# A lightning-attention and router kernel: token normalisation moved to VectorE and one step sooner, decay masks, one tile's router logits and the first head weights moved to other places in the order

## The chip, the cores and the metric

The kernel runs on one core of a Trainium2 chip. A core has a matrix engine (TensorE, "PE" in the profile, its weight loads "PEld"), VectorE ("DVE"), ScalarE ("ACT"), GpSimd ("POOL") and SyncE ("SP"), whose queue issues nearly all DMAs here. The engines run at the same time; each takes its own instructions strictly in the order of the program and waits by semaphores for the others. The metric is the device time of one execution in microseconds (us), as the median of three runs; lower is better.

## The reference, cut to what matters

Tokens are x (4 batches of 512, 512 features each), 16 heads of width 128.

```python
xn = layernorm(x)                                  # per token, no weights
q, k, v = split(silu(xn @ w_qkv.T))                # per head
for block in blocks_of_64:                         # causal, with a decay s per head
    o  = (q * exp(-s*(i+1))) @ kv + ((q @ k.T) * exp(-s*(i-j)) [i>=j]) @ v
    kv = exp(-s*64) * kv + (k * exp(-s*(63-i))).T @ v
o = norm_w * o / rms(o)
s_out = (sigmoid(xn @ w_gate.T) * o) @ w_out.T
p = softmax(xn @ router_w.T + router_b); w8, i8 = top_k(p, 8)
g = silu(xn * sum(w8) + w8 @ expert_bias[i8])
out = x + s_out * g
```

## The kernel before, in words

The program's order is written out by hand: no scheduler moves anything, so an engine's queue is exactly the order in which the functions below are called.

**Tiles and units.** The four batches form two pairs p (batches 2p and 2p+1), and 512 tokens are four tiles t of 128. So there are eight tile pairs (p, t), in the order (0,0) ... (0,3), (1,0) ... (1,3); the text numbers them 0 to 7 and writes x_n, xf_n, pt_n, lg_n for what belongs to tile pair n. The first stage computes v = silu(xn @ w_v) in 16 units k = 0 to 15: units 0 to 7 take the tile pairs with the weights of the first eight heads, units 8 to 15 take them again with those of the last eight heads, the second pair of batches first. After that come 48 head units (gate, then query and key, for each pair of batches), in which the attention of the head before is interleaved, and then the output projection.

**A unit** is a product of 2x2 blocks. `plain_unit` (units 0 and 1) does it with eight block products in four steps of two; `unit` (L480 to L517) does it with seven products (`PRODUCTS`) on sums and differences of blocks: A11·B11, S2·T2, S1·T1, A12·B21, S3·T3, S4·B22, A22·T4. A is the weight side and B the token side. These products share three accumulators in PSUM (a fourth buffer lets the next unit start). VectorE has to read an accumulator before TensorE adds to it again:

```python
            elif i == 1:
                add(temp("a"), ps, s["s1"])
            elif i == 2:
                add(temp("e"), ps, s["a"])
```

So S3·T3, which goes into the accumulator of S2·T2, waits for the addition a; S4·B22, which goes into that of S1·T1, waits for the addition e; and A22·T4 waits for the addition that follows S3·T3.

**Precision.** Each 32-bit operand is split into a high half (a rounding copy on ScalarE, `split_hi`, L100) and a low half (source minus high half, `split_lo`, L103, on VectorE or GpSimd). Each block product is then six matmuls of 128x512: two chunks of the contraction, each high·high, high·low, low·high.

**What is prepared beside the units.** `after[i]` is a list of functions that are called behind product i of the running unit, so their instructions stand there in every queue. For the tile pair of the next unit and the one after it these are: `stats` (mean and variance on VectorE, 1/std by a power on GpSimd, L234 or L238), `norms` (`normalise_x`: in place in the x tile), `turn` (eight TensorE transposes into PSUM, L262, and the copies to xf on ScalarE, L263), `sums` (four subtractions on GpSimd, L277), `plain` and `more` (the splits of the token blocks B and T, high on ScalarE, low on GpSimd), and `logits` (16 small router matmuls, L323, and an addition on VectorE, L326). In unit k they are placed as follows: `turn`, `sums`, `plain`, `more`, `logits` of tile pair k+1, `stats` and `norms` of tile pair k+2. The transposes of the next unit's tile pair thus stand right behind the first product of a unit.

`normalise_x` has two forms. Tile pairs 0 and 1 are normalised on VectorE by one instruction per batch (`normalise`, L204). The other six take a small VectorE instruction for -mean/std (`shift`, L246) and then the scaling on ScalarE (L249).

**The weights of the v stage.** `sum_of` (L441) forms S1 to S4 on VectorE from the raw weights, `split_one` splits them (in `w_A_v` and `w_S_v`). The first set is made during units 0 and 1, the second during units 3 to 8. The tiles of the sums first hold the decay tables `mkdecay` of the heads: ScalarE makes them (`make_decays`, L168), GpSimd masks them (`mask_decays`, L172), and SyncE's queue stores them to DRAM (L177); four heads share one sum's tile, and a sum can be written only when the stores of its four tables have landed.

**The weights of the heads.** The last lines of the loop open the buffers of the head stage in the space of the v stage's buffers (`vs_stack.close()`), load the raw weights of the first two head units (L421), and place the first head unit's sums and splits behind the products of unit 15 (`weight_steps`).

Of the kernel before, what the change touches and what calls it, by code (L numbers as in the profile page):

```python
# [8 lines left out]
F32 = mybir.dt.float32  # L9
F32R = mybir.dt.float32r  # L10
AF = mybir.ActivationFunctionType
ALU = mybir.AluOpType
AX = mybir.AxisListType

P = 128
# [35 lines left out]
def kernel(  # L51
# [13 lines left out]
    nc = tc.nc  # L65
# [12 lines left out]
    def pool(stack, name, bufs=1, **kw):  # L78
        return stack.enter_context(tc.tile_pool(name=name, bufs=bufs, **kw))
# [10 lines left out]
    small = pool(ctx, "small", 4)  # L90
# [75 lines left out]
    def make_decays(d, hs):  # L166
        for h in hs:
            nc.scalar.activation(d[h // 4][:, h % 4], dist, AF.Exp, scale=slopes[:, h : h + 1])  # L168

    def mask_decays(d, hs):  # L170
        for h in hs:
            nc.gpsimd.affine_select(  # L172
                d[h // 4][:, h % 4, 0], d[h // 4][:, h % 4, 0], pattern=[[1, P]],
                compare_op=ALU.is_ge, fill=0.0, base=0, channel_multiplier=-1,
            )
        for h in hs:
            nc.sync.dma_start(out=decay_d[h], in_=d[h // 4][:, h % 4])  # L177


    stats = [const.tile([P, NT, 2], F32, tag=f"stats{b}", name=f"stats{b}") for b in range(B)]  # L180
    rstd_of = [const.tile([P, NT, PB], F32, tag=f"rstd{p}", name=f"rstd{p}") for p in range(B // PB)]
    rstd = [rstd_of[b // PB][:, :, b % PB] for b in range(B)]
# [20 lines left out]
    def normalise(dst, src, b, t):  # L203
        nc.vector.tensor_scalar(  # L204
            dst, src, stats[b][:, t, 0:1], rstd[b][:, t : t + 1], ALU.subtract, ALU.mult
        )
# [8 lines left out]
    xts = {}  # L215
# [7 lines left out]
    def layer_norms(p, t, apart=False):  # L223
        var = small.tile([P, PB], F32, tag="lnvar", name=f"lnv_{p}_{t}")
        for j in range(PB):
            b = p * PB + j
            st = small.tile([P, nc.vector.BN_STATS_DIM], F32, tag="bn", name=f"bn_{b}_{t}")
            nc.vector.bn_stats(st, xts[b, t])
            nc.vector.bn_aggr(stats[b][:, t, :], st)
            nc.vector.tensor_scalar(  # L230
                var[:, j : j + 1], stats[b][:, t, 1:2], 1.0, LN_EPS, ALU.mult, ALU.add
            )
            if apart:
                nc.gpsimd.tensor_tensor(  # L234
                    rstd_of[p][:, t, j : j + 1], var[:, j : j + 1], mhalf[:, 0:1], ALU.pow
                )
        if not apart:
            nc.gpsimd.tensor_tensor(rstd_of[p][:, t], var, mhalf[:, 0:PB], ALU.pow)  # L238

    def normalise_x(p, t, vector=False):  # L240
        for b in range(p * PB, p * PB + PB):
            if vector:
                normalise(xts[b, t], xts[b, t], b, t)
                continue
            shift = small.tile([P, 1], F32, tag="shift", name=f"shift_{b}_{t}")
            nc.vector.scalar_tensor_tensor(  # L246
                shift, stats[b][:, t, 0:1], -1.0, rstd[b][:, t : t + 1], ALU.mult, ALU.mult
            )
            nc.scalar.activation(  # L249
                xts[b, t], xts[b, t], AF.Identity, bias=shift, scale=rstd[b][:, t : t + 1]  # L250
            )

    xfs = {}

# [295 lines left out]
    def nothing():  # L550
        return [[] for _ in PRODUCTS]
# [262 lines left out]
    NP_FIRST = 2  # L814

    def prepare(stage, p, t):
        first = (p, t) == (0, 0)
        early = p == 0 and t < NP_FIRST

        def turn():  # L820
            for j in range(PB):
                transpose(stage, p, j, t)
            if p == 0:
                nc.sync.dma_start(out=xf_d[t], in_=xfs[p, t])

        if p == 0 and t < NP_FIRST:
            sums = (lambda: plain(p, t, nc.vector if t == 0 else nc.gpsimd)), lambda: None, lambda: None
        else:
            sums = combine(stage, p, t, nc.gpsimd)

        def route_logits():
            logits(stage, p, t)
        return {
            "stats": lambda: layer_norms(p, t, first), "norms": lambda: normalise_x(p, t, early),
            "turn": turn, "sums": sums[0], "plain": sums[1], "more": sums[2], "logits": route_logits,
        }

# [14 lines left out]
    def weight_steps(w, after):  # L852
        for i in range(4):
            after[i // 2].append(lambda i=i: w.sum_of(i, nc.gpsimd))

        def split(i):
            if i == 0:
                w.parts = w.splits((nc.gpsimd,) * 4)
            w.parts[i]()
        for i in range(4):  # L860
            after[2 + i].append(lambda i=i: split(i))

    def load_pair(stage, p, t):
        for j in range(PB):
            load_x(stage, p * PB + j, t)
# [5 lines left out]
    stage = right(vs_stack, "stage", 4)  # L871
# [3 lines left out]
    tiles = [(p, t) for p in range(NP) for t in range(NT)]  # L875
    again = [(p, t) for p in reversed(range(NP)) for t in range(NT)]
    n1 = len(tiles)
    prep = [prepare(stage, p, t) for p, t in tiles]
# [18 lines left out]
    for n in ["A21"] + [n for n, _, _, _ in PRODUCTS]:  # L897
# [3 lines left out]
    ds = [  # L901
        sump.tile([P, KC * VW], F32, tag=f"sum{i}", name=f"mkdecay_{i}").rearrange(
            "p (h a m) -> p h a m", a=2, m=P
        ) for i in range(4)
    ]
    hs = range(0, 7), range(7, 12), range(12, NH)
# [13 lines left out]
    ws[0].split_one("A21", nc.vector)  # L920
    make_decays(ds, hs[1])
    prep[1]["norms"]()
    ws[0].split_one("A22", nc.gpsimd)
    make_decays(ds, hs[2])

    for k, (p, t) in enumerate(tiles + again):
        g, after = k // n1, nothing()
        for unit_of, what in ((n1 - 3, (0, "top")), (n1 - 2, (0, "less")), (n1 + 2, (1, "top")), (n1 + 3, (1, "less"))):
            if k == unit_of:
                after[2].append(lambda what=what: scores_less(*what))  # L930
        if n1 - NT <= k < n1:
            after[6].append(lambda p=p, t=t: keep_blocks(p, t))
        if k + 1 < n1:
            after[0 if k else 1].append(prep[k + 1]["turn"])
            if k + 3 < n1:
                after[0].append(lambda k=k: load_pair(stage, *tiles[k + 3]))
            after[1].append(prep[k + 1]["sums"])
            if k + 2 < n1:
                after[1].append(prep[k + 2]["stats"])
                after[5].append(prep[k + 2]["norms"])  # L940
            after[1].append(prep[k + 1]["plain"])
            after[4].append(prep[k + 1]["more"])
            after[4].append(prep[k + 1]["logits"])
        if k == 0:
            after[1].append(lambda: mask_decays(ds, [*hs[1], *hs[2]]))
        if k < NP_FIRST:
            for i in range(2 * k, 2 * k + 2):
                after[2 + 2 * (i % 2)].append(lambda i=i: ws[0].sum_of(i, nc.vector))
            for i, n in enumerate((("S1", "S2"), ("S3", "S4"))[k]):
                eng = nc.gpsimd if i else nc.vector  # L950
                after[2 * i + 3].append(lambda n=n, eng=eng: ws[0].split_one(n, eng))
        if k == NP_FIRST:
            after[0].append(ws[1].load())
        if n1 - 5 <= k < n1 - 1:
            after[3].append(lambda n=k - n1 + 5: ws[1].sum_of(n, nc.vector))
        for n, unit_of, step, eng, piece in (
            ("A11", n1 - 2, 6, nc.gpsimd, None), ("S2", n1 - 1, 0, nc.gpsimd, None),
            ("S1", n1 - 1, 1, nc.gpsimd, None), ("A12", n1 - 1, 2, nc.vector, 0),
            ("S3", n1 - 1, 3, nc.gpsimd, None), ("A12", n1 - 1, 4, nc.vector, 1),
            ("S4", n1, 2, nc.vector, 0), ("S4", n1, 3, nc.vector, 1), ("A22", n1, 0, nc.gpsimd, None),  # L960
        ):
            if k == unit_of:
                after[step].append(lambda n=n, eng=eng, piece=piece: ws[1].split_one(n, eng, piece))
        if n1 <= k < n1 + NT:
            after[0].append(lambda t=t: load_xf(stage, t))
        if n1 < k <= n1 + NT:
            sums, split_plain, split_sums = combine(stage, 0, k - n1 - 1, nc.gpsimd, "r")
            after[1] += [sums, split_plain]
            after[4].append(split_sums)
        if k == n1 + NT + 1:  # L970
            after[1].append(scores_exp)
        if k == 2 * n1 - 1:
            vs_stack.close()
            todo = [(p, *u) for p in range(NP) for u in h_units(p, hw_stack)]
            todo[0][3].load()()
            todo[1][3].load()()
            weight_steps(todo[0][3], after)
        v_unit(p, g, t, ws[g], vout, after, k < NP_FIRST)
    do_deferred()
# [33 lines left out]
    for i, (p, kind, n, w) in enumerate(todo):  # L1013
        after = nothing()
# [148 lines left out]
```

## Time and profile before

| what | value |
|---|---|
| median of three runs | 1091.9 us (1091.29 to 1092.09) |
| the profiled execution: its time | 1092.31 us |
| its span, first to last instruction | 1090.4 us |
| TensorE busy | 1069.5 us, 98% of the span, 5762 instructions |
| VectorE, ScalarE, GpSimd busy | 678.5, 488.7 and 720.1 us |
| mean granted TensorE clock | 0.996 of full speed |

The span and the time outside it (1.9 us) come from one execution. Busy shares are averages over stages, and an engine that is busy 98% of the time has little to lose in waits; the places where TensorE stands still can be counted one by one in the timeline. Units 0 to 15 take the first 201 us of the span.

### The profile page before, as it was taken

To read this page: it belongs to the slowest core of one execution; us is meant where nothing else is said; L and a number is where in the kernel's file an instruction comes from. 1 tells how busy PE (TensorE), PEld (TensorE's weight loads), DVE (VectorE), ACT (ScalarE), POOL (GpSimd) and SP (SyncE) were. 2 spreads that over 40 slices of the span, in tenths; PEclk is the share of its full clock that TensorE was granted. 3 is DMA by queue.
4 is the path that set the end of the run, shared out by engine and by line. 5 is a ranking of instruction groups with operands and counts; after the bars stand their busy time and mean duration, and the time that the engine had idled before them with its cause. 6 is when DMAs were issued, how large, how long until landed. Compare 5 with 4: busy or idle time off the path is not lost.

```text
span 1090.4 us, 16500 instructions
## 1 busy us (share of the span) xinstructions
PE 1069.5 (98%) x5762; PEld 912.5 (84%) x5762; DVE 678.5 (62%) x1059; ACT 488.7 (45%) x950; POOL 720.1 (66%) x725
## 2 busy tenths in 40 slices
PE   8899999999999999999999999999999999999998
PEld 7677788788888888888888888888888888788886
DVE  5677876567776655655646556556566575854554
ACT  7555555444444444444444444444444444321311
POOL 5777794777677786787777767867777756722130
PEclk9999999999999999999999999999999999999999
DMA  7465743532224223324732232223222428354351
GB/s 243 170 213 198 259 170 127 187 113 97 69 87 136 92 83 109 100 89 145 277 113 82 83 120 89 82 84 97 91 82 83 131 81 266 110 176 164 116 175 57
DMA packets 105058, 143.08 MB, mean 131 GB/s; under 512 B 9104, under 2 KB 53264, under 8 KB 104080
## 3 DMA queue, kind: packets, MB, share of 16 engines
q1 hardware_dynamic: 104112, 141.33, 39.2%
q8 instruction: 45, 0.74, 0.3%
q10 hardware_dynamic: 864, 0.70, 0.2%
q14 instruction: 37, 0.30, 0.1%
HBM read 91.14 MB, written 50.86 MB: 130 GB/s over the span
## 4 chain that ended last, share of the span: by engine, by line
PE 87%; DVE 3%; issue 1%; ACT 1%; POOL 0%; DVEq 0%; ACTq 0%; POOLq 0%
PE u_qk L505 27%; PE po L806 16%; PE u_g L505 14%; PE u_v L505 8%; PE sa L674 5%; PE o L711 5%; PE ss L697 4%; PE o L713 4%; PE kt L677 2%; PE pu L766 1%; DVE q L561 0%; PE ssq L738 0%; DVE k L561 0%; DVE w_S_v L103 0%; POOL sqs L723 0%
## 5 line engine op out<-in xcount | busy, mean ns | idle before, releaser
L806 PE MATMUL po<-wr,yr 128*128 128x512 f32 x768 | 181.1, 394 | 1.5 <-DVE u L800 1.5
L806 PEld LDWEIGHTS po<-wr,yr 128*128 128x128 f32 x768 | 144.8, 189 | 33.2 <-ACT yr L100 1.9
L505 PE MATMUL u_qk<-blk_T,ws_qk 128*128 128x512 f32 x576 | 150.2, 400 | 0.0
L723 POOL TENSOR_TENSOR sqs<-sqs,sq 128x512 f32<-128x512 f32 x60 | 77.3, 1288 | 91.4 <-ACT sq L722 89.8
L505 PEld LDWEIGHTS u_qk<-blk_T,ws_qk 128*128 128x128 f32 x576 | 104.8, 189 | 20.8
L701 DVE SCALAR_TENSOR_TENSOR st<-st,bdecay,ss 128x128 f32<-128x128 f32 x128 | 44.4, 348 | 106.2 <-ACT st L699 104.0
L505 PE MATMUL u_qk<-blk_B,wa_qk 128*128 128x512 f32 x384 | 100.7, 397 | 0.0
L103 DVE TENSOR_TENSOR yr<-yin,yr 128x512 fp32r<-128x512 f32 x64 | 69.2, 1116 | 46.5 <-ACT yr L100 44.6
L103 POOL TENSOR_TENSOR ws_qk<-sum_qk,ws_qk 128x512 fp32r<-128x512 f32 x64 | 87.9, 1384 | 14.6 <-ACT ws_qk L100 14.5
L711 PE MATMUL o<-at,vin 128*128 128x128 f32 x512 | 88.3, 274 | 0.0
L505 PEld LDWEIGHTS u_qk<-blk_B,wa_qk 128*128 128x128 f32 x384 | 71.0, 188 | 15.3
L711 PEld LDWEIGHTS o<-at,vin 128*128 128x128 f32 x512 | 77.3, 191 | 5.5
L505 PE MATMUL u_g<-blk_T,ws_g 128*128 128x512 f32 x288 | 78.4, 407 | 0.0
L683 ACT ACTIVATE kd<-kt,kdecay 128x384 f32<-128x384 f32 x64 | 37.2, 582 | 90.3 <-PE kt L677 90.3
L713 PE MATMUL o<-qd,st 128*128 128x128 f32 x384 | 74.2, 275 | 0.0
L715 DVE SCALAR_TENSOR_TENSOR y<-o,nw,gt 128x512 f32<-128x512 f32 x64 | 47.9, 749 | 40.8 <-PE o L713 39.6
L674 PEld LDWEIGHTS sa<-q,k 128*128 128x128 f32 x512 | 66.8, 191 | 7.6 <-DVE q L561 2.0
L558 ACT ACTIVATE sg_k<-k 128x512 f32<-128x512 f32 x64 | 40.5, 633 | 65.3 <-DVE k L496 65.3
L770 POOL TENSOR_TENSOR u<-u,sgu 128x512 f32<-128x512 f32 x16 | 20.7, 1292 | 73.5 <-ACT sgu L769 60.2
L674 PE MATMUL sa<-q,k 128*128 128x128 f32 x512 | 67.7, 275 | 1.2 <-DVE q L561 1.1
L685 POOL TENSOR_TENSOR qd<-q,dec 128x384 f32<-128x384 f32 x64 | 65.5, 1025 | 0.0
L722 ACT ACTIVATE sq<-o 128x512 f32<-128x512 f32 x60 | 35.9, 598 | 62.7 <-DVE y L715 58.1
(184 smaller groups left out, 2455.2 us busy)
## 6 DMA issues: line engine op xcount, KB each, us to landing
v<-vo_v SPq DMA_DIRECT2D x64, 256.0 KB, 2.1
raw_qk<-in_w_head_dram SPq DMA_DIRECT2D x64, 256.0 KB, 3.7
vin<-v SPq DMA_DIRECT2D x64, 256.0 KB, 3.3
y<-y SPq DMA_DIRECT2D x64, 256.0 KB, 2.1
yin<-y SPq DMA_DIRECT2D x64, 256.0 KB, 3.5
x<-in_x_dram SPq DMA_DIRECT2D x32, 256.0 KB, 4.9
raw_g<-in_w_head_dram SPq DMA_DIRECT2D x32, 256.0 KB, 3.2
raw_v<-in_w_v_dram SPq DMA_DIRECT2D x16, 256.0 KB, 5.7
```

The costliest lines, as they stand in the source:

```text
L103: eng.tensor_tensor(lo, src, hi.bitcast(F32), ALU.subtract)
L505: nc.tensor.matmul(ps, lhsT, rhs, start=(first and c == 0 and n == 0), stop=(c == KC - 1 and n == len(PASSES) - 1), skip_group_check=not f ...
L558: nc.scalar.activation(sg, src, AF.Sigmoid)
L674: nc.tensor.matmul(pa[:, c], k[:, c], q[:, c], start=True, stop=True)
L685: nc.gpsimd.tensor_tensor(qd[s], q[:, 1:], d[:, 1, None, :].to_broadcast([P, NT - 1, P]), ALU.mult)
L697: nc.tensor.matmul(ps[:, c], kd[s][:, c], v_of(b, h, c), start=True, stop=True)
L701: nc.vector.scalar_tensor_tensor(r[:, c], r[:, c - 1], bdecay[:, h : h + 1], ps[:, c], ALU.mult, ALU.add)
L711: nc.tensor.matmul(o, v_of(b, h, c), at[s][:, c], start=True, stop=(c == 0))
L713: nc.tensor.matmul(o, st[s][:, c - 1], qd[s][:, c - 1], start=False, stop=True)
L715: nc.vector.scalar_tensor_tensor(y, po, nw[:, h : h + 1], gts[s], ALU.mult, ALU.mult)
L723: nc.gpsimd.tensor_tensor(sq[b], sq[b], s1, ALU.add)
L806: nc.tensor.matmul(pos[t], yr[:, yi, bass.ts(t, P)], wos[h][:, wi], start=(h == 0 and n == 0), stop=(h == NH - 1 and n == len(PASSES) - 1),)
```

## The change

1. `normalise_x` always uses VectorE (`normalise`); the form with `shift` and ScalarE goes. For tile pairs 2 to 7, `norms` moves from `after[5]` to `after[4]` of unit k, ahead of `more` and `logits`.
2. The masks and the stores of the decay tables of heads 7 to 15 move from unit 0 (behind its step of two products) to before the units: those of heads 7 to 11 ahead of the low half of A22, those of heads 12 to 15 behind it. The loads of x_3 are called ahead of them (in SyncE's queue these loads stay where they were), and nine stores now stand ahead of the first two stores of unit 0.
3. The router logits of tile pair 1 move in unit 0 from `after[4]` to `after[6]`, behind the unit's last two products.
4. The low half of S4 of the second weight set moves in unit 8 from behind products 2 and 3 to behind products 0 and 1.
5. The head stage's buffers are opened, and the first two head units' raw weights loaded, in unit 14; the first head unit's sums and splits stay in unit 15.

```diff
-    def normalise_x(p, t, vector=False):
+    def normalise_x(p, t):
         for b in range(p * PB, p * PB + PB):
-            if vector:
-                normalise(xts[b, t], xts[b, t], b, t)
-                continue
-            shift = small.tile([P, 1], F32, tag="shift", name=f"shift_{b}_{t}")
-            nc.vector.scalar_tensor_tensor(
-                shift, stats[b][:, t, 0:1], -1.0, rstd[b][:, t : t + 1], ALU.mult, ALU.mult
-            )
-            nc.scalar.activation(
-                xts[b, t], xts[b, t], AF.Identity, bias=shift, scale=rstd[b][:, t : t + 1]
-            )
+            normalise(xts[b, t], xts[b, t], b, t)
...
     prep[1]["norms"]()
+    load_pair(stage, *tiles[3])
+    mask_decays(ds, hs[1])
     ws[0].split_one("A22", nc.gpsimd)
     make_decays(ds, hs[2])
+    mask_decays(ds, hs[2])
...
-            if k + 3 < n1:
+            if 0 < k < n1 - 3:
                 after[0].append(lambda k=k: load_pair(stage, *tiles[k + 3]))
             after[1].append(prep[k + 1]["sums"])
             if k + 2 < n1:
                 after[1].append(prep[k + 2]["stats"])
-                after[5].append(prep[k + 2]["norms"])
+                after[4].append(prep[k + 2]["norms"])
             after[1].append(prep[k + 1]["plain"])
             after[4].append(prep[k + 1]["more"])
-            after[4].append(prep[k + 1]["logits"])
-        if k == 0:
-            after[1].append(lambda: mask_decays(ds, [*hs[1], *hs[2]]))
+            after[4 if k else 6].append(prep[k + 1]["logits"])
...
-            ("S4", n1, 2, nc.vector, 0), ("S4", n1, 3, nc.vector, 1), ("A22", n1, 0, nc.gpsimd, None),
+            ("S4", n1, 0, nc.vector, 0), ("S4", n1, 1, nc.vector, 1), ("A22", n1, 0, nc.gpsimd, None),
...
-        if k == 2 * n1 - 1:
+        if k == 2 * n1 - 2:
             vs_stack.close()
             todo = [(p, *u) for p in range(NP) for u in h_units(p, hw_stack)]
             todo[0][3].load()()
             todo[1][3].load()()
+        if k == 2 * n1 - 1:
             weight_steps(todo[0][3], after)
```

More of the change, by code (lines that the diff above doesn't have):

```diff
@@ L817, in prepare @@
         first = (p, t) == (0, 0)
-        early = p == 0 and t < NP_FIRST
         def turn():
@@ L833, in prepare @@
         return {
-            "stats": lambda: layer_norms(p, t, first), "norms": lambda: normalise_x(p, t, early),
+            "stats": lambda: layer_norms(p, t, first), "norms": lambda: normalise_x(p, t),
             "turn": turn, "sums": sums[0], "plain": sums[1], "more": sums[2], "logits": route_logits,
```

## The prediction

> **What bounds the kernel now.** I read the page's busy line first, then TensorE's waits, then its timeline, then those of the engines that it waits for. Lines of the page and of TensorE's waits (sum, times, longest, in us):
>
> ```profile
> PE 1069.5 (98%) x5762; PEld 912.5 (84%) x5762; DVE 678.5 (62%) x1059; ACT 488.7 (45%) x950; POOL 720.1 (66%) x725
> ...
> PE pt L262 <- ACT x L249: 7.2, 6, 3.2
> PE lg L323 <- ACT xf L263: 1.9, 2, 1.5
> ...
> PE u_v L505 <- DVE w_S_v L103: 0.9, 2, 0.7
> PE u_g L505 <- POOL wa_g L103: 0.7, 1, 0.7
> ```
>
> TensorE sets the end; whatever it does not wait for is worth nothing. Nearly all its waits are in the v stage, and the largest name the normalised x. The timeline of TensorE (start, length; the end of the one before can overlap) prices them:
>
> ```profile
> 20.04 1.53 PE L537 MATMUL d_v<-w_A_v,blk_T 128*128 128x512 f32 x6
> 23.04 2.00 PE L323 MATMUL lg<-rw,xf 128*128 128x64 f32 x16 [1.47 <-ACT xf L263]
> ...
> 29.04 1.52 PE L537 MATMUL d_v<-w_A_v,blk_T 128*128 128x512 f32 x6
> 33.81 1.97 PE L262 MATMUL pt<-ident,x 128*128 128x128 f32 x8 [3.25 <-ACT x L249]
> ...
> 46.15 1.52 PE L505 MATMUL u_v<-w_A_v,blk_B 128*128 128x512 f32 x6
> 49.06 1.36 PE L262 MATMUL pt<-ident,x 128*128 128x128 f32 x8 [1.39 <-ACT x L249]
> ...
> 128.72 1.57 PE L505 MATMUL u_v<-w_S_v,blk_T 128*128 128x512 f32 x6
> ```
>
> Six 128x512 matmuls take 1.36 us start to start, so each stall is the distance between two starts less 1.36: lg_1 23.04-20.04 gives 1.64; pt_2 33.81-29.04 gives 3.41; pt_3 1.55; pt_4 to pt_7, read in the same way (62.38-60.27, 75.82-73.59, 89.25-87.03, 102.52-100.46), 0.75+0.87+0.86+0.70 = 3.18. Unit 8: from S3's start at 128.72 to the next unit's at 134.76 is 6.04 where three products take 4.08: 1.96. First gate unit: 2.34 for a first product of 1.40 and 3.10 for the next two, of 2.80: 1.24. One more cost has no wait beside it: by windows (PE, PEld, DVE, ACT, POOL busy, then clock, DMA)
>
> ```profile
> 29.97:33.39 3.42, 0.59 (x3) 0.17 (x1) 2.42 (x5) 0.45 (x1) 1.00 (x5) 1.00 0.81 265
> 33.39:36.80 3.41, 2.99 (x11) 2.76 (x12) 0.14 (x1) 3.01 (x5) 1.32 (x2) 0.50 0.83 303
> ```
>
> the granted clock falls to 0.50 right behind pt_2's stall. From 33.81 to 41.62 lie the transposes (1.12 elsewhere) and 24 matmuls (5.44): 7.81 instead of 6.56, so 1.25.
>
> All that the change can reach is 1.64+3.41+1.25+1.55+3.18+1.96+1.24 = 14.2 us.
>
> **The change part by part.**
>
> *lg_1 behind the unit's last products.* It goes to a place where xf_1 (ready 23.47) has long been copied: TensorE reaches it at 21.41+2.72 = 24.1. A22 now follows at 21.41; its low half on GpSimd ended at 21.12. Gain 1.64.
>
> *Masks.* Five masks at 0.245 us (nine took 2.25) come in front of that low half. GpSimd was idle from 16.99 to 18.58, until A22's high half was cast, and ScalarE has made these five tables by 17.57; they end at 18.2, hidden. Without that gap A22 would wait up to 1.2. The other four (1.0 us) fall into 21.12 to 23.85, also idle. The nine stores take 0.40 to 0.49 each of SyncE's queue, at about 19.4 to 23.7 instead of 29.04 to 33.29; behind them the store of the first v tile leaves a microsecond late (23.8 for 22.77), and its buffer is not written again before 33. What goes is VectorE's wait of 1.97 for its second weight sum (`mkdecay`, until 30.97).
>
> *x_2.* VectorE's order is now: S1's low half (ends 28.80), normalise twice, the second sum. 1/std is there at 28.76. One normalisation took 0.54, so the two batches are ready at 29.4 and 29.85 instead of 34.47. TensorE, 1.64 earlier, would be free at 30.40-1.64 = 28.76: 0.65 of 3.41 stays, gain 2.76. With no stretch of TensorE nearly idle for 3.4 us the slow clock goes too. The Trainium skill ("TensorE: Matmul & The Clock Gate", Part 1) says that an idle window of about 3.4 us puts TensorE at half rate for the next, on windows that run freely: by that rule 1.7 lost and gained, by the rows 1.25. I take 1.25. A later half-clock window (910.6) depends on where windows fall; I count nothing for it.
>
> *x_3 to x_7.* Each pair of `shift` (0.38 on average) and of scalings (0.80 on ScalarE) becomes a pair of normalisations on VectorE one product earlier. In units 3 to 6 VectorE was idle for 1.14 just there (before the addition behind S4·B22), x is ready some 3 us before its transposes, and the accumulators that the delayed additions free are not wanted for 3 more. So 3.18, and up to 1.55 in unit 2.
>
> *What comes next there* is GpSimd and VectorE in units 1 to 3. GpSimd worked from S2's low half (35.48) to T2's of tile pair 3 (59.6) with 1.66 idle: 22.5 us. S2's low half now starts at 29.8+1.22 (sum)+1.05 (cast) = 32.1, so T2 is ready at 54.6. Unit 3 starts, with all gains, at 60.27-7.20 = 53.07 and wants T2's low half 1.36+1.12+0.23 later, at 55.8. Here a rule speaks against the change: the Trainium skill ("SBUF — State Buffer", "SBUF: two separate sides") says that VectorE, when it reads through two ports, and GpSimd hold one port pair exclusively, for a whole instruction. The row of the only normalisations that ran beside GpSimd:
>
> ```profile
> L204 DVE TENSOR_SCALAR u<-x,stats,rstd x16: 533/538/1510, 922.4 to 1067.5; 128x512 f32<-128x512 f32 x16
> ```
>
> The median 0.54 is a free one, the 1.51 one that waited. By the median alone GpSimd loses nothing and T2 is in time; by the rule each of four normalisations takes some 0.4 from GpSimd, T2 comes at 56.2. And it waits for GpSimd in turn: x_3 stands behind the sum (1.23), the cast (1.05) and S3's two low halves (1.9) from 36.3 on, is ready between 41.5 (free) and 43.2 (each waits once), and is wanted at 41.8 and 42.4. Loss 0 to 3 in all. VectorE's 42 products of two SBUF tiles in this stage took 0.68 to 1.78, 0.91 on average, those with one tile in PSUM never over 0.70; that is nearer to the rule than to no lock, so I take 1.5. By the median alone the sum below would be 11.6.
>
> *S4 in unit 8.* VectorE, its row and the two beside it:
>
> ```profile
> 127.90 0.68 DVE L496 TENSOR_TENSOR a_v<-u_v,s_v 128x512 f32<-128x512 f32 x1
> 128.68 0.69 DVE L496 TENSOR_TENSOR e_v<-u_v,a_v 128x512 f32<-128x512 f32 x1
> 129.29 3.33 DVE L103 TENSOR_TENSOR w_S_v<-sum_v,w_S_v 128x512 fp32r<-128x512 f32 x2
> ```
>
> The two pieces, 1.65 each beside a busy GpSimd, now stand ahead of a and ahead of e. VectorE comes to them at 127.98, GpSimd is in S3's low half until 129.13, so the first ends at about 129.7, a at 130.3, the second at 131.5, e at 132.1. S3·T3 waits for a: 130.3 instead of 128.72. S4·B22 waits for e: 132.2. A22 ends at 134.9, where the unit ended at 134.76. The stall is not removed but moves from S4 to S3, because a is late next. Bounds: 0.9 lost (both pieces at 1.76 and no overlap) to 1.96 gained; I take 0.
>
> *Head weights.* Four loads (0.42 each) leave at 184.3 instead of 193.79, ahead of one store of v, which comes 1.5 later and whose buffer is free until 194. They land near 188; GpSimd, idle until 198.00, makes the sums; ScalarE casts wa_g behind its copy that ends at 194.05, and the low half is ready near 196, wanted at 201.9. Gain 1.24.
>
> **Sum**, against the profiled execution's 1092.31: 1.64+2.76+1.25+1.55+3.18+0+1.24-1.5 = 10.1, so 1082.2. It lies 0.4 above the runs' median, which gives 1091.9-10.1 = **1081.8 us**, 0.9% faster.
>
> **The rivals.**
>
> *Everything goes.* No lock, and S4's pieces are early enough: 14.2 at most, 12.6 without the 0.65 and half of the S4 term: 1079.3. For it: most rows at free durations. Against: a cannot be earlier than the piece ahead of it. Chance 0.15.
>
> *Waits that take the place of the ones removed.* In units 1 to 6 the low halves on GpSimd, held up by VectorE's new reads, become the bound, and transposes or products wait for them: pt_3's 1.55 and half of the 3.18 stay under other names, and 1.5 more is lost than I take. Left 10.1-1.55-1.6-1.5 = 5.45: 1086.4. For it: GpSimd was busy 18.34 of 20 us between 40 and 60. Against: idle stretches of 3 to 3.7 us per unit from unit 3 on. This is also the case in which the change does not do what it says. Chance 0.2.
>
> *Slower.* A normalisation stands in VectorE's queue ahead of additions that free accumulators, and waits for 1/std from GpSimd. In units 3 to 6 1/std was ready 2.1 us ahead of that place (68.73 for 70.9), and the additions have 3.1 more. If GpSimd's chain came 7 us later each time, each of six units would lose 1.8, 10.8 in all, and cancel the 10.1; at 8 us it is 6x2.8 = 16.8 and the time 1098.6. The deciding point is a 1/std that lands 7 us later against VectorE; the profile shows locks of 0.5 to 1.2. Chance 0.05.
>
> **How the numbers follow.** Forecast as summed (8 to 12 us): 0.58; everything goes 0.15; other waits 0.2; slower 0.05; no difference 0.02. What a measurement here can tell from no change is about 0.2%, 2.2 us. Faster: 0.58+0.15+0.2 = 0.93; same 0.02; slower 0.05. The range: down to 14.2 less the fixed 0.65, 1078.3, and up to the middle case's 1086.4: 1078.3 to 1086.4.
>
> **What would show it.** Right: TensorE's waits name no x behind ScalarE; no half clock near 33; lg_1 without a wait; from units 3 to 6 a period of 12.6 instead of 13.4; GpSimd's weight sums without the wait of 21.6 near 198; in unit 8 S3's product late instead of S4's. Wrong: TensorE waiting for low halves from GpSimd (blk_B, blk_T, w_S_v) in units 1 to 6, or normalisations of 1.0 to 1.5 throughout.

## The result, and the profile after

The changed kernel takes 1074.5 us (median of 6 runs, 1073.68 to 1075.04) where the kernel before, in the same session, took 1092.0 (1091.29 to 1094.77): ratio 0.984, 95% interval 0.982 to 0.985, so 1.6% faster. The forecast was 1081.8, with a range of 1078.3 to 1086.4. The direction was right, the gain of 10.1 us was too small by 7.4.

The page's busy line of the kernel after:

```profile
PE 1058.8 (99%) x5762; PEld 909.6 (85%) x5762; DVE 686.3 (64%) x1059; ACT 479.8 (45%) x938; POOL 724.2 (67%) x725
```

TensorE has 10.7 us less busy time for the same 5762 instructions. An instruction that waits isn't busy, so of the waits only those short enough to hide under the length of the instruction before can be in that figure, and the slow clock was put at only 1.25. By windows 4.5 of the 10.7 lie in the head stage. So part of the gain is not what the change was read for. TensorE's waits (sum, times, longest, us):

```profile
PE pt L253 <- DVE x L204: 2.7, 5, 1.0
...
PE u_v L496 <- DVE a_v L487: 1.2, 1, 1.2
...
PE u_v L496 <- DVE vo_v L552: 0.2, 1, 0.2
```

The waits for ScalarE's x (7.2), for w_S_v (0.9) and for wa_g (0.7) are gone. The normalised x is now VectorE's (two of its five waits, 1.4 together, are those of the first tile pair, ahead of unit 0), and one wait for `a` in unit 8 is new. (The lines of the file after are 9 lower than before from `normalise_x` on: L262 is now L253, L505 is L496.)

TensorE's timeline in units 0 to 3 (start, length, instruction, in brackets the wait):

```profile
24.36 1.89 PE L314 MATMUL lg<-rw,xf 128*128 128x64 f32 x16
...
29.89 1.08 PE L253 MATMUL pt<-ident,x 128*128 128x128 f32 x8 [0.77 <-DVE x L204]
...
36.27 1.89 PE L314 MATMUL lg<-rw,xf 128*128 128x64 f32 x16
...
42.31 0.63 PE L253 MATMUL pt<-ident,x 128*128 128x128 f32 x4
43.19 0.63 PE L253 MATMUL pt<-ident,x 128*128 128x128 f32 x4 [0.25 <-DVE x L204]
...
45.36 1.66 PE L496 MATMUL u_v<-w_S_v,blk_T 128*128 128x512 f32 x6 [0.15 <-DVE vo_v L552]
...
54.13 1.52 PE L496 MATMUL u_v<-w_A_v,blk_B 128*128 128x512 f32 x6
55.50 1.03 PE L253 MATMUL pt<-ident,x 128*128 128x128 f32 x8
56.29 3.00 PE L496 MATMUL u_v<-w_S_v,blk_T 128*128 128x512 f32 x12
```

lg_1 goes through without a wait. pt_2 still waits 0.77, and pt_3 0.25 for its second batch. From unit 3 on (the last three rows) the transposes start 1.37 behind the product ahead of them, with no stall. The slow stretch behind pt_2 is gone too; this is the window (PE, PEld, DVE, ACT, POOL busy, then clock, DMA share, GB/s) that answers to the one at 0.50:

```profile
29.50:33.00 3.50, 3.11 (x18) 2.73 (x19) 3.23 (x6) 1.64 (x3) 0.51 (x1) 1.00 0.06 22
```

Where the 17.45 us between the two profiled spans (1090.44 and 1072.99) lie is read by following the same instruction in both timelines and subtracting the starts:

| stretch, up to the start of | before | after | gain in it | predicted |
|---|---|---|---|---|
| A22·T4 of unit 2 | 58.91 | 52.75 | 6.16 | 5.70 |
| A22·T4 of unit 7 | 121.90 | 111.33 | 4.41 | 3.18 |
| first gate unit | 201.43 | 190.74 | 0.12 | 0 |
| first q/k unit | 212.47 | 200.26 | 1.52 | 1.24 |
| last sum of squares, end of the 48 head units | 908.68 | 892.40 | 4.07 | 0 |
| end of the span | 1090.44 | 1072.99 | 1.17 | 0 |

5.70 is 1.64+2.76+1.25+1.55 less the 1.5 for the port. The largest miss is in the head units, where I had no term at all. Nothing waits less there; the matmuls are shorter. The first q/k unit before:

```profile
212.47 1.56 PE L505 MATMUL u_qk<-blk_B,wa_qk 128*128 128x512 f32 x6
213.87 2.96 PE L505 MATMUL u_qk<-blk_T,ws_qk 128*128 128x512 f32 x12
```

and after:

```profile
200.26 1.52 PE L496 MATMUL u_qk<-blk_B,wa_qk 128*128 128x512 f32 x6
201.62 2.88 PE L496 MATMUL u_qk<-blk_T,ws_qk 128*128 128x512 f32 x12
```

Six matmuls take 1.40 start to start before and 1.36 after. Matmul by matmul the step in this unit is 229 and 237 ns in turn before, 233 on average, and 227 after. Of the 336 products of the head stage, 148 follow directly on another product: their step went from 232 to 227.5. The 188 that follow on matmuls of attention gained less (233 to 231, their first step left out). The order of TensorE's instructions in the head stage is the same in both kernels, and so is its granted clock (1.00).

### The profile page after: what moved, and what is told of

Its sections match the earlier page's. It is cut to its first block, busy times and chain, and to the rows that moved or that the text cites. A ratio compares the mean times of both kernels' runs of the same rounds, so it can differ in the third digit from the quotient of the medians.

```text
span 1073.0 us, 16479 instructions
## 1 busy us (share of the span) xinstructions
PE 1058.8 (99%) x5762; PEld 909.6 (85%) x5762; DVE 686.3 (64%) x1059; ACT 479.8 (45%) x938; POOL 724.2 (67%) x725
## 4 chain that ended last, share of the span: by engine, by line
PE 91%; DVE 5%; ACT 2%; DMA 1%; issue 1%; POOL 0%; SPq 0%; DVEq 0%; ACTq 0%; POOLq 0%
PE u_qk L496 27%; PE po L797 16%; PE u_g L496 14%; PE u_v L496 11%; PE sa L665 5%; PE o L702 5%; PE ss L688 4%; PE o L704 4%; PE kt L668 2%; DMA raw_v<-in_w_v_dram 1%; DVE vo_v L552 1%; PE lg L314 1%; PE pu L757 1%; DVE sum_v L432 1%; ACT w_A_v L100 0%
## 5 line engine op out<-in xcount | busy, mean ns | idle before, releaser
L496 PE MATMUL u_qk<-blk_T,ws_qk 128*128 128x512 f32 x576 | 149.1, 398 | 0.0
L496 PEld LDWEIGHTS u_qk<-blk_T,ws_qk 128*128 128x128 f32 x576 | 104.7, 188 | 20.3
L496 PE MATMUL u_qk<-blk_B,wa_qk 128*128 128x512 f32 x384 | 99.6, 395 | 0.0
L496 PEld LDWEIGHTS u_qk<-blk_B,wa_qk 128*128 128x128 f32 x384 | 70.8, 188 | 14.3
L496 PE MATMUL u_g<-blk_T,ws_g 128*128 128x512 f32 x288 | 77.8, 406 | 0.0
L496 PE MATMUL u_v<-w_S_v,blk_T 128*128 128x512 f32 x252 | 62.7, 392 | 1.3 <-DVE a_v L487 1.2
```

The source lines that it names most:

```text
L496: nc.tensor.matmul(ps, lhsT, rhs, start=(first and c == 0 and n == 0), stop=(c == KC - 1 and n == len(PASSES) - 1), skip_group_check=not f ...
```

## The experiments

One thing that no line of the diff names does change in the head stage: where tiles lie. The four 4-byte `shift` tiles took 32 bytes per partition each, in the pool of small tiles. They are gone, so all that is allocated behind them on that side lies 128 bytes lower: the blocks of x (the head units' moving operand) went from 34656 to 34528, from 42848 to 42720, and so on. The head units' weights (the stationary operand) lie on the other side of the memory and stayed at 188384 and up. In the addresses that the compiled kernels have, modulo 256, blocks and weights stood at 96 and 224 before and stand at 224 and 224 after. In the v stage it is the blocks that are stationary and the v weights that move. Both lie behind `shift`, so their distance did not change, and the step there is 227 in both kernels.

**Theory 1:** the head stage's gain is this shift. **Rival:** something else that the change moved, or the chip.

### The 128 bytes alone, put into the kernel after and taken from the kernel before

```diff
 # e1: after, plus
+nc.gpsimd.memset(small.tile([P, 1], F32, tag="shift", name="pad_0"), 0.0)
 # e2: before, with
-shift = small.tile([P, 1], F32, tag="shift", name=f"shift_{b}_{t}")
+shift = rms[b][:, t : t + 1]
```

> The kernel after, with four unused tiles of 32 bytes put back where the four `shift` tiles lay, so that everything allocated behind them (the blocks of x, the v weights, v's output tiles, the stage of the projection) lies 128 bytes higher, as in the kernel before. Nothing else differs but four... one GpSimd fill of one such tile at the start. Theory 1 (addresses): TensorE's 512-column matmuls of the head units go back from 227 ns to 231-237 ns a step, 3.5 to 4.1 us are lost between the first q/k product and the last head, time 1078.0 to 1078.6. Rival (the step is set by something else that the change moved, or by the chip): step 227 ns as in the kernel after, time 1074.5 within 0.7.

> The kernel before, in which `shift` is written into a column of a table that exists anyway and is filled only at the end (rms), so that the four `shift` tiles go and all that lies behind them moves down by 128 bytes, as in the kernel after. No instruction is added, removed or moved. Theory 1 (addresses): the head units' step falls from 231-237 ns to 227 ns, time 1092.0 - 3.9 = 1088.1 (1087.5 to 1088.7). Rival: 1092.0 within 0.7.

Measured: e1 1079.85 us (ratio to before 0.989, 0.987 to 0.991), e2 1087.06 (0.996, 0.995 to 0.997). On e1's chip the places of the kernel after took 1074.41 (e4, below). The kernel after lost 5.35 by a fill of one unused tile (its pool keeps four buffers of 32 bytes for it, which makes the 128), the kernel before gained 4.7 with no instruction added or moved (`shift` only goes to another place). Both moved by more than was expected of the head stage alone; the rest is found below, in the first gate unit and the projection. The first q/k unit of e1, then of e2:

```profile
199.73 1.56 PE L498 MATMUL u_qk<-blk_B,wa_qk 128*128 128x512 f32 x6
201.12 2.96 PE L498 MATMUL u_qk<-blk_T,ws_qk 128*128 128x512 f32 x12
```

```profile
211.55 1.52 PE L505 MATMUL u_qk<-blk_B,wa_qk 128*128 128x512 f32 x6
212.91 2.88 PE L505 MATMUL u_qk<-blk_T,ws_qk 128*128 128x512 f32 x12
```

Each has taken the other kernel's lengths. Theory 1 stands, and the rival falls.

### Which places matter: four more pads, and the weights alone

```diff
 # e5: after, plus 128 unused bytes first on the other side (weights, q, k, v in, y move; blocks stay)
+nc.gpsimd.memset(right(ctx, "rpad").tile([P, 32], F32, tag="rpad", name="rpad"), 0.0)
 # e6: e5's pad, and 128 bytes ahead of the blocks.  e7: 256, e8: 32, e12: 64 bytes ahead of the blocks (no other pad)
+nc.gpsimd.memset(small.tile([P, 32], F32, tag="shift", name="pad", bufs=1), 0.0)
 # f1: 128 unused bytes on both sides of the head units' weight pool
-for n, k in (("raw", 2), ("sum", 1), ("w", 2))
+for n, k in (("raw", 2), ("sum", 1), ("pad1", 1), ("w", 2), ("pad2", 1))
```

> The kernel after with an unused tile of 128 bytes at the start of the right side of SBUF: the head units' weights (the stationary operand), q, k, v in and y lie 128 bytes lower, the blocks of x of the first pair of batches (the moving operand) stay. Theory 1a (the place of the moving rows themselves decides: 224 within 256 bytes is fast, 96 is slow): the first 24 units keep 227 ns as in the kernel after; in the last 24 the four blocks that lie on the right side turn slow; 1074.5 to 1077. Theory 1b (the distance between moving rows and weights decides: equal places within 256 bytes are fast, 128 bytes apart slow): all of the first 24 units turn to 231-237 ns, and the last 24 are mixed as in the kernel before; 1079 to 1080.

> Both pads at once: the blocks of x 128 bytes higher and the weights 128 bytes lower, so that the two stand to each other (within 256 bytes) as in the kernel after, but the blocks of the first pair of batches lie where they lay in the kernel before. Theory 1a (place of the moving rows): slow everywhere, in the last 24 units too, 1080 to 1082. Theory 1b (distance): 227 ns as in the kernel after, 1074.5 within 1.

> The kernel after with an unused tile of 256 bytes ahead of the blocks: all that lies behind moves up by 256. If only the place within 256 bytes counts (1a and 1b alike): 227 ns, 1074.5 within 1. If the place within 512 bytes or the address as such counts: slower, up to 1080.

> The kernel after with an unused tile of 32 bytes ahead of the blocks: the moving rows begin at a multiple of 256, and stand 32 bytes off the weights' place. If equal places are needed: slower, up to 1080. If only a distance near 128 is bad: 1074.5 within 1. If a row that begins at a multiple of 256 is read faster than one that begins 32 before it: faster than 1074.5, and the gate units' 231 ns fall.

> The kernel after with an unused tile of 64 bytes ahead of the blocks of x: moving rows and weights stand 64 bytes apart within 256. If only equal places within 256 bytes are fast: head units at 231-237 ns, 1079 to 1081. If equal places within 64 bytes were enough, this would be fast, 1074.5, but the 128 bytes of the first runs speak against it.

> The kernel after with unused tiles of 128 bytes on both sides of the head units' weight tiles: only these (the stationary operand) lie 128 bytes lower within 256, while the blocks, q, k, v in, y and the tiles of the projection stage keep their places. If the pair is moving rows and stationary weights: all 48 head units at 231-237 ns, the projection stage unchanged, time 1074.5 + 3.7 and something more for the units of the second pair of batches that stayed fast so far: 1078 to 1081. If the pair is another (blocks against q, k, v in or y): 1074.5 within 1.

The head stage is read as the start of the last sum of squares less that of the first q/k product; the step is the mean over the first q/k unit:

| kernel | blocks / weights, mod 256 | step in the first q/k unit, ns | head stage, us | time, us |
|---|---|---|---|---|
| before | 96 / 224 | 233 | 696.2 | 1092.0 |
| after | 224 / 224 | 227 | 692.1 | 1074.5 |
| e1 | 96 / 224 | 232 | 696.1 | 1079.85 |
| e2 (order of before) | 224 / 224 | 227 | 692.1 | 1087.06 |
| e5 | 224 / 96 | 232 | 696.0 | 1079.76 |
| e6 | 96 / 96 | 227 | 692.2 | 1074.73 |
| e7 | 224 / 224 | 227 | 692.3 | 1074.75 |
| e8 | 0 / 224 | 233 | 696.7 | 1080.8 |
| e12 | 32 / 224 | 229 | 693.9 | 1076.69 |
| f1 | 224 / 96, in all 48 units | 232 | 697.5 | 1080.34 |

e5 and e6 decide between the place itself and the distance: with the blocks where the kernel after has them the stage is slow as soon as the weights move away (e5), and with the blocks where the kernel before has them it is fast when the weights move along (e6). So it is the distance between moving rows and weights, modulo 256 bytes (e7: 256 more is no change). 0 apart is fast, 128 and 32 apart are slow, and 64 apart costs somewhat less than half (1.7 of 4.1), which neither of e12's two expectations had. Other distances were not tried. f1 moves nothing but the weights, modulo 256; the tiles of attention and of the projection keep their places. Its first q/k unit:

```profile
200.41 1.56 PE L496 MATMUL u_qk<-blk_B,wa_qk 128*128 128x512 f32 x6
201.80 2.96 PE L496 MATMUL u_qk<-blk_T,ws_qk 128*128 128x512 f32 x12
```

So the pair is the matmul's two operands. f1 is also the only one that slows all 24 units of the second pair of batches: there four of the seven blocks lie on the weights' side and move with them in the other kernels, which is why the kernel before ran only its T3, B22 and T4 products slow in them. Counted so, before has 24x42 + 24x18 = 1440 slow matmuls, and 4.07 us are 2.8 ns each on average; f1 has 2016, and 697.5-692.1 = 5.4 us are 2.7 each.

The projection stage shows the same. There the tokens y are stationary and w_out moves; from the second batch on y lies on the right side, and the w_out tiles of the first four heads lie behind the blocks of x, so that their distance follows that of the blocks. In the 144 matmuls of these heads and batches the step is 233 ns in the four kernels with 128 or 32 bytes between (before, e1, e5, e8), 229 at 64 (e12), and 227 in all others; with the other twelve heads it is 227 in every kernel. That is 0.94 of the last 1.17 of the table. Head stage (4.07), first gate unit (0.24 by e1) and projection (0.94) together make 5.25, which is what e1 lost.

Left open: by what mechanism the two reads disturb each other, and why products that follow on matmuls of attention stay near 231 ns with equal places too.

### The normalisations: ScalarE again, and VectorE at the old place

```diff
 # e3: after, tokens 2 to 7 as in the kernel before (scaling on ScalarE, shift kept in rms), and
-after[4].append(prep[k + 2]["norms"])
+after[5].append(prep[k + 2]["norms"])
 # e11: after, with this line alone
```

> The kernel after with tokens 2 to 7 normalised by ScalarE again, one product later as in the kernel before, `shift` kept in a column of rms so that no address moves. By the prediction's terms (2.76 + 1.25 + 1.55 + 3.18 - 1.5 = 7.24) the time is 1081.7. If each stall costs some 0.33 more than its wait, because the product behind it starts late too, and the port lock costs 0.5 and not 1.5, TensorE's v stage loses 10.7 - 1.6 = 9.0 and the time is 1083.5. In both the head units keep 227 ns.

> The kernel after with tokens 2 to 7 normalised on VectorE, but one product later, as ScalarE's were in the kernel before. Tells the engine from the place: if the place carries the gain, the time is that of the run with ScalarE, 1083.2; if the engine carries it, 1074.5. In units 3 to 6 ScalarE's x came 0.75 to 0.87 late at this place; two normalisations of 0.95 on VectorE behind the addition against two scalings of 0.80 on ScalarE would come at about the same time: 1080 to 1083.

Measured: e3 1083.2 us (0.992, 0.991 to 0.993), e11 1078.78 (0.988, 0.986 to 0.990). By the start of the first gate unit e3 has lost 8.1 to the kernel after, and e11 3.4. So of the 8.1 some 4.7 belong to the engine and 3.4 to the place (by the medians 4.4 and 4.3); e3 came as its second expectation said, and e11 was expected slower than it came. The 4.7 hold a slow clock: e3's execution has 0.50 from 31.38 to 34.80, behind pt_2's stall as in the kernel before, and from pt_2 to lg_2 it takes 1.56 more than the kernel after; e11's has none. e3 in unit 3, to be set beside the rows at 54.13 to 56.29:

```profile
57.57 1.52 PE L505 MATMUL u_v<-w_A_v,blk_B 128*128 128x512 f32 x6
59.65 1.37 PE L262 MATMUL pt<-ident,x 128*128 128x128 f32 x8 [0.56 <-ACT x L249]
60.77 3.01 PE L505 MATMUL u_v<-w_S_v,blk_T 128*128 128x512 f32 x12
```

The eight transposes start 2.08 behind the product where the kernel after has 1.37, a stall of 0.71; and the next product starts 1.12 behind them, where the kernel after has 0.79. These 0.33 are a second stall in the middle of the group: four transposes take 0.45, one of ScalarE's scalings takes 0.8, so the second batch's x is late once more. Matmul by matmul, in unit 4, the fourth transpose starts at 73.45 and the fifth at 73.77, where the step is 0.11 elsewhere. From A22·T4 of unit 2 to that of unit 6 the loss grows by 4.4, about 1.1 in each unit.

### S4's two low pieces

```diff
 # e4: after, old place               # e9: after, one unit sooner
-("S4", n1, 0, nc.vector, 0), ("S4", n1, 1, nc.vector, 1)
+("S4", n1, 2, nc.vector, 0), ("S4", n1, 3, nc.vector, 1)               # e4
+("S4", n1 - 1, 5, nc.vector, 0), ("S4", n1 - 1, 6, nc.vector, 1)       # e9
```

> The kernel after with the two low pieces of S4 back behind the third and fourth product of unit 8. By the prediction the move is worth 0 (the stall only changes its place from S3 to S4): 1074.5. If the move gained or lost, up to 1.96 slower or 0.9 faster.

> The kernel after with the two low pieces of S4 one unit sooner, behind the sixth and seventh product of unit 7, where their buffer is free since the fifth. If unit 8's stall stands only because the pieces stand ahead of a and e on VectorE, S3 and S4 both go through without a wait and the time is 1074.5 - 1.5 = 1073.0 (up to 2.0 gained, 1072.5). If VectorE or GpSimd is what is short there, the stall only moves again (to the additions that free the accumulators): 1074.5 or more.

In the kernel after, VectorE around the start of unit 8, and TensorE:

```profile
118.16 0.68 DVE L103 TENSOR_TENSOR w_S_v<-sum_v,w_S_v 128x512 fp32r<-128x512 f32 x1
118.76 0.68 DVE L487 TENSOR_TENSOR a_v<-u_v,s_v 128x512 f32<-128x512 f32 x1
119.36 1.15 DVE L103 TENSOR_TENSOR w_S_v<-sum_v,w_S_v 128x512 fp32r<-128x512 f32 x1
120.44 0.68 DVE L487 TENSOR_TENSOR e_v<-u_v,a_v 128x512 f32<-128x512 f32 x1
```

```profile
119.49 1.67 PE L496 MATMUL u_v<-w_S_v,blk_T 128*128 128x512 f32 x6 [1.15 <-DVE a_v L487]
121.26 1.62 PE L496 MATMUL u_v<-w_S_v,blk_B 128*128 128x512 f32 x6
```

The stall has gone from S4·B22 to S3·T3, which waits for the addition behind the first piece. Back at the old place (e4) the time is 1074.41, the same; through units 7 and 8 e4 is 0.16 ahead of the kernel after. One unit sooner (e9) it is 1075.8 (1074.36 to 1077.32), no gain, and TensorE shows why:

```profile
117.82 1.66 PE L496 MATMUL u_v<-w_A_v,blk_B 128*128 128x512 f32 x6 [1.45 <-ACT s_v L502]
```

A piece of 1.1 us now stands on VectorE ahead of an addition; ScalarE's sigmoid waits for that addition, ScalarE's copy of the next first product stands behind the sigmoid in its queue, and the fourth product of unit 8 waits for the copy. From A22·T4 of unit 7 to the first gate unit e9 loses 1.2 against the kernel after. The stall only moves, as its second expectation said.

### The head's first weights, and the logits and masks, at their old places

```diff
 # e10: after, the two loads of the head's first weights in unit 15
-if k == 2 * n1 - 2:
+if k == 2 * n1 - 1:
 # f3: after, as in the kernel before
-after[4 if k else 6].append(prep[k + 1]["logits"])
+after[4].append(prep[k + 1]["logits"])
+if k == 0: after[1].append(lambda: mask_decays(ds, [*hs[1], *hs[2]]))   # not ahead of the units
```

> The kernel after with the first head units' weights loaded in unit 15 again. By the prediction 1.24 is lost, at the first gate unit alone: 1075.75. By the landmarks of the two traces up to 1.5: 1076.0. If the early loads cost v's stores something, less than 1.24.

> The kernel after with the second tile's logits behind the fifth product of unit 0 again, and the masks of the later heads and the load of token tile 3 back in unit 0. By the prediction's first term the logits' wait costs 1.64, and the masks in their old place make VectorE's second weight sum wait some 2 us, with x of token tile 2 behind it: TensorE, 1.64 later, would wait for x 0.65 + 2.0 - 1.6 = about 1 more. So 1076.1 by the first term alone, up to 1077.2 with the second.

> The kernel after, unchanged, beside the others on the same chip: 1074.5 within 0.7.

e10 took 1075.12 (1074.29 to 1076.72), f3 1076.68 (1076.11 to 1078.17), and f2, the kernel after on f3's chip, 1075.33 (1075.30 to 1075.72), 0.8 above the first measurement; so much can lie between chips. The profiled execution of e10 lost 1.94 in the first gate unit:

```profile
192.15 1.20 PE L496 MATMUL u_g<-blk_B,wa_g 128*128 128x512 f32 x4 [1.30 <-POOL wa_g L103]
193.19 3.23 PE L496 MATMUL u_g<-blk_T,ws_g 128*128 128x512 f32 x12
```

e2, which has this load at the same place, lost only 0.57 there (10.09 for the unit where the kernel after takes 9.52). So this wait differs by more than a microsecond between kernels that load at the same place, and e10's times, which spread over 2.4 us, can't tell 1.24 from 0.6.

f3 lost 1.35 in time against f2, which is near the first term's 1.64, but 2.84 in its profiled execution by the first gate unit. It moves logits and masks together, and its transposes of pt_2 wait for nothing, so what the masks' place is worth alone is not shown. TensorE's wait for the logits is there as before, and by windows it is followed by something that the kernel before didn't have there:

```profile
24.10 2.41 PE L314 MATMUL lg<-rw,xf 128*128 128x64 f32 x16 [1.71 <-ACT xf L254]
```

```profile
22.00:25.40 3.40, 1.69 (x14) 1.30 (x12) 2.22 (x5) 3.39 (x9) 0.67 (x2) 1.00 0.34 124
25.40:28.80 3.40, 3.40 (x13) 2.92 (x12) 2.77 (x6) 1.39 (x3) 3.40 (x5) 0.52 0.39 155
```

A half-clock stretch from 25.52 to 28.94: six 128x512 matmuls at some 427 ns (one at 572) for 227, and the last logits' matmuls at 214 for 112. That is some 1.7 us in this one execution. The kernel before has nearly the same wait for the logits (1.47) and no such stretch behind it. e2 has both cases in one execution:

```profile
28.68:32.09 3.41, 1.64 (x8) 1.02 (x6) 1.45 (x3) 0.00 (x0) 2.04 (x9) 1.00 0.59 194
32.09:35.50 3.41, 1.90 (x12) 1.53 (x13) 1.18 (x4) 2.81 (x4) 0.28 (x1) 1.00 0.90 312
...
45.75:49.16 3.41, 1.70 (x12) 1.04 (x10) 2.53 (x5) 2.06 (x3) 3.29 (x4) 1.00 0.22 83
49.16:52.58 3.42, 3.42 (x10) 2.69 (x9) 0.53 (x1) 2.76 (x7) 2.94 (x3) 0.50 0.46 166
```

TensorE is busy for about half of the 3.41 us in both, and only the second is followed by half clock. So whether a stall of this size brings half clock is not fixed by the stall, nor by the busy share, and an execution's time depends on it; that fits f3's spread of 2 us, but only one execution has a trace, so of the others it isn't shown.

### One batch on each engine

```diff
 # f4: after, for tokens 2 to 7, and S4 at the old place
+if b % 2 == 0 or (p, t) in ((0, 0), (0, 1)): normalise(...)     # VectorE
+else: shift = rms[b][:, t : t + 1]; ...; nc.scalar.activation(...)   # ScalarE
```

> The kernel after with one batch of each pair normalised on VectorE and the other on ScalarE at the same place (tokens 2 to 7), and S4's pieces at the old place. If the rest of the wait in units 1 and 2 (0.77 + 0.27 at the transposes, some 0.4 at T2's low half) comes from two normalisations standing one behind the other and holding GpSimd: 0.5 to 1.3 gained, 1073.2 to 1074.0. If ScalarE, which has shift and casts ahead of it, brings the second x later than VectorE did: 1074.5 or slower, up to 1077.

1076.38 us (1075.83 to 1077.08), slower than f2 on the same chip by 1.05. By the first gate unit it is 1.1 behind the kernel after: its second batch waits 0.25 for ScalarE in pt_2 and 0.66 in pt_3. The first expectation falls, the second holds. None of these variants beats the kernel after by more than the spread of its runs (e4, 0.1 below it, is nearest).

## Why the prediction was wrong, step by step

**The sum had no term for where tiles lie.** This is the step that failed. "All that the change can reach is ... 14.2" counted waits, a slow clock and durations as fixed; the pair of `shift` instructions was removed in the sum, and the four tiles were not. Taking away 4x32 bytes is worth 4.7 to 5.35 us by e2 and e1, of which 4.07 lie in the head stage and 0.94 in the projection, in matmul steps. Without it the kernel is at 1079.85 (e1): the change that I read made 12 of the 17.5.

**x_3 to x_7: the mechanism was right, the term mis-sized.** I took 3.18 from the distance between the last product and the first transpose. The next rows, which I used as the transposes' normal length ("1.12 elsewhere"), held a second stall, since the pair's second x was late as well: unstalled they take 0.79. Four times 1.1 is 4.4, and 4.43 were gained in units 3 to 6.

**The port lock: the rule showed, its price was oversized.** The normalisations after (min/median/max ns):

```profile
L204 DVE TENSOR_SCALAR x<-x,stats,rstd x16: 534/952/1124, 6.9 to 89.2; 128x512 f32<-128x512 f32 x16
L204 DVE TENSOR_SCALAR u<-x,stats,rstd x16: 532/536/1523, 905.8 to 1050.1; 128x512 f32<-128x512 f32 x16
```

The median in the v stage is 0.95 where a free one takes 0.54. Of these, the pair of unit 1 ran while GpSimd was idle (29.16 to 32.49), that of unit 2 beside it:

```profile
29.20 1.00 DVE L204 TENSOR_SCALAR x<-x,stats,rstd 128x512 f32<-128x512 f32 x2
...
41.20 1.83 DVE L204 TENSOR_SCALAR x<-x,stats,rstd 128x512 f32<-128x512 f32 x2
```

So these rows agree with the Trainium skill ("SBUF — State Buffer", "SBUF: two separate sides") that the two engines hold each other up. What it cost TensorE is another matter. From pt_3 to A22·T4 of unit 2 the kernel after takes 10.44 where the kernel before takes 9.85, and at pt_3 it had gained 1.43 instead of 1.55: 0.71 lost, not 1.5. How much of that is the lock and how much VectorE's own queue is not shown. Nor is it lost where I put it. No product waits for T2's low half from GpSimd; the waits name VectorE (x at 43.19, vo_v at 45.36).

**pt_2 and the clock.** pt_2 starts 3.92 sooner, predicted 4.40; its x came at 29.74 for the 29.4 that I had. From pt_2 to lg_2 1.43 is gained, 1.25 predicted for the clock: the 1.12 that I took for eight transposes at full clock holds the second stall of the later units, and here they take 0.84. No half clock is left near 33.

**Right as they stood.** lg_1: no wait, at 24.36 for 24.1, and f3, which moves the masks too, gives 1.35 in time for its 1.64. S4: worth nothing, the stall on S3 because of `a`; 119.49 is 1.35 later than 1.36 behind the product ahead of it (116.78), and S4·B22 is 0.41 late after that. The head's weights: the wait is gone, 1.52 gained in that unit, of which the shorter step makes 0.24 (so much more e1 and e5 need for the unit), so near the 1.24 between these two executions; e2 and e10 show that this wait isn't the same in each. The unit period from unit 3 on is 12.26 for the 12.6 that I had said, again the 0.33.

Of the rivals, "everything goes" (1079.3) was nearest. That is no support for its reasons (no lock, S4 early enough), which both failed; even it had to stop at 1078.3, because every case was built from the same list of waits.

## What to carry to other kernels

Removing or adding a small tile moves everything allocated behind it. Before forecasting, list the addresses that a change shifts, and compare the places of each matmul's two operands modulo 256 bytes; a pad of a few bytes tests it in one run. Price a stall from the last free instruction to the next free one, not to the first that waits, because a group can stall again inside. A stall that has several pieces of work ahead of it in an in-order queue need not go by reordering them: in unit 8 three placements of the same two pieces came out equal within their spread.

## What the runs showed of the hardware, unexpected

- The step of a 128x512 matmul with 32-bit operands depends on the distance between its moving rows and its weights in SBUF, modulo 256 bytes: 227 ns at equal places, 229 at 64 bytes apart, 232 to 233 at 128 and 233 at 32, read in the first q/k unit and, with other tiles, in the projection. The Trainium skill ("TensorE: Matmul & The Clock Gate", "Step-by-step: what each phase is for") says that loading the next weights doesn't take read bandwidth from the running matmul; these runs, in which nothing but the weights' place moved (f1, 5.4 us), show that the two operands' places do matter together, and the measurement decides. That the loading of weights is what disturbs the rows is not shown.
- Half clock followed a stretch of 3.4 us in which TensorE was busy for 1.7 (f3, and e2 at 45.75), so not only an idle one, and another with 1.64 (e2 at 28.68) was followed by full clock. The rule that I weighed (the same page, Part 1) speaks of an idle window, on windows that run freely; what it counts as idle these traces don't tell, but it isn't the profile's busy share.
